# A third room for residual rows, a second for transposed probabilities, four other pairs for M, and tile 5's split between two exponentials

## The chip, the cores and the metric

The kernel runs on one core of one Trainium2 chip. A core has five engines, each working through its own list of instructions in order: TensorE (PE, with its weight loads, PEld), VectorE (DVE), ScalarE (ACT), GpSimd (POOL) and SyncE (SP), which here does little but issue DMAs. An engine that comes to an instruction whose operands are not there waits, and all that stands behind it in its list waits too. The metric is the device time of one execution in microseconds. Three runs before the change took 957.74, 960.12 and 963.96 us; the median is 960.12.

## What is computed

A block of four residual layers on x, 2 batches of 1024 tokens with 512 features, all in float32:

```python
x = x + attn_a(layernorm(x))    # gated linear attention in chunks of 128, 4 heads, state carried over chunks
x = x + ffn(layernorm(x))       # (silu(x Wg) * (x Wu)) Wd, hidden size 1408, integer weights with scales
x = x + attn_b(layernorm(x))    # softmax(Q K^T / sqrt(512)) V Wo, one head of width 512
x = x + ffn(layernorm(x))       # the same weights again
```

Of attention a, only the output is used. For each tile of 128 tokens it needs q, a normalised k and v, the decays from the gates, the scores inside the tile, and the state from the tiles before.

## The kernel before

**Tiles and precision.** The 2048 tokens are 16 tiles of 128. Matmuls take operands in a rounded form of float32 (fp32r). To keep float32 precision an operand is held as a high and a low part: `split` (lines 83 to 86) lets ACT cast to the high part and DVE, or POOL, subtract it from the source to get the low part. `mm3` (lines 97 to 103) then does three matmuls: high by high, high by low, low by high.

**Attention a** (lines 349 to 753). Before its loop the weights of attention b are folded into products: M from W_q and W_k at the start (`weight_product`, name "M"), and V from W_v and W_o near the end. M comes out of PE in four PSUM blocks. `spill` (line 181) splits each block and stores both parts in DRAM, where attention b fetches them; its tiles come from a pool under a given tag. Then q of four tiles (`q_head`, one head at a time), layer norms with transposes (`ln_tile`), and v of tile 0. The loop over 16 tiles does `kv_tile` (k and v of the next tile, tags sWk and sWv), `scores` (k transposed as kT, the state's update pd from kw and v, then the scores pS) and `chunk_out` (output of the tile before, with a residual row xra). `k_norm` and `k_factor` turn k into kw: square on ACT, sum on DVE, a power on POOL, factors on DVE, the product on POOL. `decay` reads a row from DRAM (`load_row`) and masks it on POOL.

**FFN** (line 756 on). Pairs of hidden blocks use a seven-product scheme with combined operands (B11, T1, T2 and so on, prepared from the transposed tokens by `combine`).

**Attention b** (lines 896 to 1187). For each batch, four cycles: `scores_head`, then work in between, then `scores_tail` with `softmax` for two tiles. `probs_T` transposes the probabilities: DVE transposes blocks of 32 by 32 into py, a DMA writes py to DRAM (p), four DMAs read it back placed into ptl, and `probs_split` splits it into pth and ptl for `out_b`. The tile before the last is transposed on PE instead (ppt). Tile numbers in the profile: tiles 8 to 15 belong to batch 1, so tile 13 is its tile 5.

**Order.** Tile pools hold a number of rooms (bufs) per tag, and a new tile takes the room of the one that many tiles before it; whoever writes it waits until the old tile's last user is done. Row tiles (tag xres) have two rooms, py one, sWk two. A scheduler in the program's builder puts each engine's instructions in order by its own estimate of times; `behind(...)` only says that a step is not to be issued ahead of given instructions. SP's list of DMAs is ordered in this way too, so a load whose room is not free holds up all later DMAs of SP.

## Time and profile before

| | us |
|---|---|
| median of three runs | 960.12 |
| profiled execution | 960.54 |
| its span, first to last instruction | 958.8 |
| PE busy in the span | 936.6 |
| DVE busy | 728.9 |
| ACT busy | 408.6 |
| POOL busy | 222.1 |

The profiled execution has 1.74 us around its span, and lies 0.42 us over the median. PE is busy for 98% of the span. Its matmuls overlap in the records: one of 128 by 512 lasts 0.39 us but the next starts 0.23 us after it. In the lists of waits a line names the waiting engine, tile and line, and what released it, with the total, the number and the longest wait. In the chain of work that ended last, a line has its start, its length, and the engine and tile. In the windows, a line gives for each engine the busy time and the number of instructions, then the granted clock of PE (1.00 is full), the DMA share and the rate in GB/s. A bracket at the end of a line of the timeline is idle time before it.

### The profile page before, as it was taken

How to read it: one execution, taken by the hardware profiler on the slowest of the kernel's cores; microseconds unless marked ns; L12 is line 12 of the kernel's file. 1: busy time of each engine (PE TensorE's matmuls, PEld its weight loads, DVE VectorE, ACT ScalarE, POOL GpSimd, SP SyncE). 2: the span in 40 equal slices, each digit the busy share in tenths (PEclk: the TensorE clock that was granted, in tenths of full speed). 3: DMA queues.
4: the chain of work that ended last, by engine and by line, in shares of the span. 5: the costliest groups of instructions: out<-in, count | busy, mean ns of one | idle time of the engine just before them, and what ended most of it. 6: DMA issues, size and time to landing. Idle time of an engine off the chain costs nothing.

```text
span 958.8 us, 13209 instructions
## 1 busy us (share of the span) xinstructions
PE 936.6 (98%) x4402; PEld 776.3 (81%) x4402; DVE 728.9 (76%) x1457; ACT 408.6 (43%) x793; POOL 222.1 (23%) x318
## 2 busy tenths in 40 slices
PE   8979999998899999999999999999999999999998
PEld 6768888887788878888888888888878888888887
DVE  7656767677999799787956897658975977976655
ACT  5543343425566443444324444234532444534421
POOL 6223322333464110210030400222400261001100
PEclk9999999999999999999999999999999999999999
DMA  8335546664798538652560787516877772573112
GB/s 298 110 132 140 167 112 185 178 150 148 290 387 245 170 124 310 183 150 67 198 216 12 165 198 173 190 22 132 195 173 235 280 209 52 180 263 132 39 59 96
DMA packets 215861, 162.18 MB, mean 169 GB/s; under 512 B 150960, under 2 KB 166640, under 8 KB 215792
## 3 DMA queue, kind: packets, MB, share of 16 engines
q1 hardware_dynamic: 213488, 156.61, 53.7%
q0 software_dynamic: 2304, 4.72, 2.3%
q8 instruction: 35, 0.57, 0.3%
q14 instruction: 34, 0.28, 0.1%
HBM read 104.76 MB, written 41.84 MB: 153 GB/s over the span
## 4 chain that ended last, share of the span: by engine, by line
PE 81%; DVE 7%; DMA 6%; ACT 2%; issue 1%; POOL 1%; SPq 1%; ACTq 0%; DVEq 0%; POOLq 0%
PE pog L868 4%; PE pog L867 4%; PE pZg L339 4%; PE pVg L339 4%; PE pXg L339 4%; PE pVf L339 4%; PE pZf L339 3%; PE pXf L339 3%; PE pob L100 3%; PE pof L867 3%; PE pob L98 3%; PE pob L99 3%; PE pof L868 3%; PE pYg L339 2%; PE psV L965 2%; PE psZ L965 2%
## 5 line engine op out<-in xcount | busy, mean ns | idle before, releaser
L867 PE MATMUL pog<-wdg,hsg 128*128 128x512 f32 (+1 forms) x165 | 60.1, 375 | 0.0
L868 PE MATMUL pog<-wdg,hsg 128*128 128x512 f32 (+1 forms) x165 | 60.1, 375 | 0.0
L868 PE MATMUL pof<-wdf,hsf 128*128 128x512 f32 x154 | 59.3, 390 | 0.8 <-DVE ve_b L121 0.8
L867 PE MATMUL pof<-wdf,hsf 128*128 128x512 f32 x154 | 59.1, 389 | 0.0
L98 PE MATMUL pob<-vh,pth 128*128 128x512 f32 x128 | 50.7, 396 | 1.2 <-ACT pth L85 1.2
L100 PE MATMUL pob<-vh,ptl 128*128 128x512 f32 x128 | 50.6, 396 | 0.7 <-DVE ptl L86 0.7
L99 PE MATMUL pob<-vl,pth 128*128 128x512 f32 x128 | 50.4, 394 | 0.0
L86 POOL TENSOR_TENSOR hsg<-sgg,hsg 128x128 fp32r<-128x128 f32 x40 | 17.6, 460 | 130.0 <-ACT hsg L85 130.0
L339 PE MATMUL pVg<-T_g,wcg 128*128 128x512 f32 x176 | 46.6, 389 | 0.0
L339 PE MATMUL pVf<-T_f,wcf 128*128 128x512 f32 x176 | 46.6, 389 | 0.0
L339 PE MATMUL pXg<-B_g,wcg 128*128 128x512 f32 x176 | 46.4, 389 | 0.0
L339 PE MATMUL pXf<-B_f,wcf 128*128 128x512 f32 x176 | 46.0, 390 | 0.3 <-DMA wcf<-wc 0.3
L123 POOL TENSOR_TENSOR rs_g<-ve_g,mhalf 128x1 f32<-128x1 f32 x16 | 13.2, 828 | 139.2 <-DVE ve_g L121 139.2
L123 POOL TENSOR_TENSOR rs_b<-ve_b,mhalf 128x1 f32<-128x1 f32 x16 | 11.3, 709 | 140.5 <-DVE ve_b L121 140.5
L211 POOL DMA_DIRECT2D xT_g<-y_g x48 | 30.9, 651 | 36.7 <-DVE T_b L86 28.7
L339 PEld LDWEIGHTS pXf<-B_f,wcf 128*128 128x128 f32 x176 | 32.9, 188 | 7.4 <-DMA wcf<-wc 0.7
L339 PEld LDWEIGHTS pVg<-T_g,wcg 128*128 128x128 f32 x176 | 33.0, 188 | 6.9
L339 PEld LDWEIGHTS pXg<-B_g,wcg 128*128 128x128 f32 x176 | 33.0, 188 | 6.9
L339 PEld LDWEIGHTS pVf<-T_f,wcf 128*128 128x128 f32 x176 | 33.0, 188 | 6.9
L867 PEld LDWEIGHTS pog<-wdg,hsg 128*128 128x128 f32 x165 | 31.1, 188 | 5.7
L868 PEld LDWEIGHTS pog<-wdg,hsg 128*128 128x128 f32 x165 | 31.0, 188 | 5.6
L868 PEld LDWEIGHTS pof<-wdf,hsf 128*128 128x128 f32 x154 | 28.9, 188 | 7.2 <-DVE hsf L86 1.2
(334 smaller groups left out, 2740.4 us busy)
## 6 DMA issues: line engine op xcount, KB each, us to landing
wcg<-wc SPq DMA_DIRECT2D x22, 896.0 KB, 6.3
wc<-wcf SPq DMA_DIRECT2D x11, 896.0 KB, 5.2
wcf<-wc SPq DMA_DIRECT2D x11, 896.0 KB, 6.0
p<-py SPq DMA_DIRECT2D x15, 512.0 KB, 3.7
ptl<-p SPq DMA_DIRECT2D x56, 128.0 KB, 3.0
xin_a<-in_x SPq DMA_DIRECT2D x16, 256.0 KB, 4.0
xra<-in_x SPq DMA_DIRECT2D x16, 256.0 KB, 2.7
row<-cl SPq DMA_DIRECT2D x16, 256.0 KB, 3.6
```

The source lines that it names most:

```text
L86: return c.ins, (eng or nc.vector).tensor_tensor(lo, src, hi.bitcast(F32), ALU.subtract).ins
L98: nc.tensor.matmul(ps, lhs_hi, rhs_hi, start=first, stop=False)
L99: nc.tensor.matmul(ps, lhs_hi, rhs_lo, start=False, stop=False)
L100: end = nc.tensor.matmul(ps, lhs_lo, rhs_hi, start=False, stop=last).ins
L123: nc.gpsimd.tensor_tensor(rs, ve, mhalf, ALU.pow)
L211: (nc.sync if sync else nc.gpsimd).dma_start(out=xf[32 * b : 32 * (b + 1), :, c, :], in_=y[32 * c : 32 * (c + 1), b].rearrange("p k i q -> ...
L339: nc.tensor.matmul(ps, w[:, m, k * P : (k + 1) * P], o[:, s, k, :], start=first and k == 0 and s == 0, stop=k == 1 and s == 1, skip_group_ ...
L867: nc.tensor.matmul(ps, hs[i][0][:, j], wd[j][:, ds], start=j == 0, stop=False)
L868: nc.tensor.matmul(ps, hs[i][1][:, j], wd[j][:, ds], start=False, stop=j == KH - 1)
L965: ends[nm] = nc.tensor.matmul(ps, o[:, i, k], w[:, j, k], start=first and k == 0 and i + j == 0, stop=k == 1 and i == 1, skip_group_check= ...
```

## The change

Eight things are altered.

1. Residual rows get a pool of their own with three rooms, for all four layers.
2. py gets two rooms instead of one.
3. `spill` of M uses the tags kT, kw, sdec and at (two rooms each) instead of sWk.
4. The layer norms of tiles 4 to 7 stand behind the q heads: none after the first, then 4, 5, and 6 with 7.
5. For batch 1's tile 5, `probs_split` moves out of the cycle into `scores_tail`, after the first tile's softmax; the second tile's exponentials are to stand behind its casts.
6. Two steps of the second FFN's operands (`do(moving, 2)`) move from ahead of the last cycle into it.
7. s3 takes the room of u2; the gate tile ab gets one room.
8. Constants used by attention a alone go into attention a's pool.

```diff
+    rp = ctx.enter_context(tc.tile_pool(name="rows", bufs=3))
...
-        xin = xp.tile([P, D], F32, tag=tag, name=f"xin_{name}")
+        xin = (rp if tag == "xres" else xp).tile([P, D], F32, tag=tag, name=f"xin_{name}")
...
-            ab = ap.tile([48, 512], F32R, tag="ab", name=f"ab{st}")
+            ab = a1.tile([48, 512], F32R, tag="ab", name=f"ab{st}")
...
-            xr = xp.tile([P, D], F32, tag="xres", name=f"xra{t}")
+            xr = rp.tile([P, D], F32, tag="xres", name=f"xra{t}")
...
-        spill(ap, ("sWk",), pm, m_d, "M")
+        spill(ap, ("kT", "kw", "sdec", "at"), pm, m_d, "M")
         for i in range(4):
+            ends.clear()
             q_head(0, i)
-            with behind((wq_loaded,)):
-                ln_tile(4 + i)
+            with behind((wq_loaded, *ends.values())):
+                for t in ((), (4,), (5,), (6, 7))[i]:
+                    ln_tile(t)
...
-            s3 = b1.tile([P, 2, P], F32, tag="s3", name=f"s3_{b}{n}")
+            s3 = b1.tile([P, 512], F32, tag="u2", name=f"s3_{b}{n}")
+            s3 = s3[:, 0:256].rearrange("p (k c) -> p k c", k=2)
...
             softmax(b * NK + 2 * n, (X, Z))
-            softmax(b * NK + 2 * n + 1, (V, up))
+            casts = []
+            if (b, n) == (1, 3):
+
+                casts = probs_split(1, 5, last)
+            softmax(b * NK + 2 * n + 1, (V, up), casts)
...
             for s, x in enumerate(halves):
-                act = nc.scalar.activation(
-                    pe[:, s * 512 : (s + 1) * 512], x, AF.Exp, bias=nm, scale=SC, accum_out=rs[:, s : s + 1]
-                )
+                with behind(casts):
+                    act = nc.scalar.activation(
+                        pe[:, s * 512 : (s + 1) * 512], x, AF.Exp, bias=nm, scale=SC, accum_out=rs[:, s : s + 1]
+                    )
...
-            y = b1.tile([P, T], F32, tag="py", name=f"py{t}")
+            y = bp.tile([P, T], F32, tag="py", name=f"py{t}")
...
                 for i in (2 * n - 2, 2 * n - 1):
-                    probs_split(b, i, summed)
+                    if (b, i) != (1, 5):
+                        probs_split(b, i, summed)
...
-            if b:
-                do(moving, 2)
-            else:
+            if b == 0:
                 moving = combine("b", 1)
                 do(moving, 1)
-            cycle(b, 3, lambda: out_b(b, 3))
+
+            def between():
+                out_b(b, 3)
+                if b:
+                    with behind(summed):
+                        do(moving, 2)
+
+            cycle(b, 3, between)
```

The row tiles of the FFN (xrf, xrg) and of attention b (xrb) change in the same way as xra. The scheduler orders the changed program anew, so instructions stand elsewhere too where no line was edited.

More of the change, by code (lines that the diff above doesn't have):

```diff
@@ L55, in hybrid_block_kernel @@
     make_identity(nc, ident)
-    ones = cp.tile([P, P], F32, name="ones")
-    nc.gpsimd.memset(ones, 1.0)
-    le = cp.tile([P, P], F32, name="le")
-    nc.gpsimd.affine_select(
-        out=le, in_=ones, compare_op=ALU.is_ge, fill=0.0, base=0, pattern=[[1, P]], channel_multiplier=-1
-    )
-    gt = cp.tile([P, P], F32, name="gt")
-    nc.vector.tensor_tensor(gt, ones, le, ALU.subtract)
-    fold_f = cp.tile([48, 8], F32, name="fold_f")
-    nc.vector.tensor_reduce(
-        fold_f, ident[0:48, 0:64].rearrange("p (a b c) -> p c a b", a=2, b=4)[:, :, :, 0:2], AX.XY, ALU.add
-    )
-    fold = cp.tile([48, 8], F32R, name="fold")
-    nc.vector.tensor_copy(fold, fold_f)
     mhalf = cp.tile([P, 1], F32, name="mhalf")
@@ L353, in hybrid_block_kernel @@
         sp = actx.enter_context(tc.tile_pool(name="stage", bufs=4))
+        ones = a1.tile([P, P], F32, name="ones")
+        nc.gpsimd.memset(ones, 1.0)
+        le = a1.tile([P, P], F32, name="le")
+        nc.gpsimd.affine_select(
+            out=le, in_=ones, compare_op=ALU.is_ge, fill=0.0, base=0, pattern=[[1, P]], channel_multiplier=-1
+        )
+        gt = a1.tile([P, P], F32, name="gt")
+        nc.vector.tensor_tensor(gt, ones, le, ALU.subtract)
+        fold_f = a1.tile([48, 8], F32, name="fold_f")
+        nc.vector.tensor_reduce(
+            fold_f, ident[0:48, 0:64].rearrange("p (a b c) -> p c a b", a=2, b=4)[:, :, :, 0:2], AX.XY, ALU.add
+        )
+        fold = a1.tile([48, 8], F32R, name="fold")
+        nc.vector.tensor_copy(fold, fold_f)
         normed, key_copy, late_norm = {}, [], []
@@ L858, in ffn @@
                             done = h_split(n, js, ha[:, n - 2, js] if n < ST else hb[:, n - ST, js], None)
-                    xr = xp.tile([P, D], F32, tag="xres", name=f"xr{nm}{t}")
+                    xr = rp.tile([P, D], F32, tag="xres", name=f"xr{nm}{t}")
                     nc.sync.dma_start(out=xr, in_=src[t])
@@ L993, in scores_tail, with softmax @@
             softmax(b * NK + 2 * n, (X, Z))
-            softmax(b * NK + 2 * n + 1, (V, up))
-        def softmax(t, halves):
+            casts = []
+            if (b, n) == (1, 3):
+                casts = probs_split(1, 5, last)
+            softmax(b * NK + 2 * n + 1, (V, up), casts)
+        def softmax(t, halves, casts=()):
             mx = mp.tile([P, 2], F32, tag="mx", name=f"mx{t}")
@@ L1004, in softmax @@
             for s, x in enumerate(halves):
-                act = nc.scalar.activation(
-                    pe[:, s * 512 : (s + 1) * 512], x, AF.Exp, bias=nm, scale=SC, accum_out=rs[:, s : s + 1]
-                )
+                with behind(casts):
+                    act = nc.scalar.activation(
+                        pe[:, s * 512 : (s + 1) * 512], x, AF.Exp, bias=nm, scale=SC, accum_out=rs[:, s : s + 1]
+                    )
             ri = mp.tile([P, 1], F32, tag="ri", name=f"ri{t}")
@@ L1053, in probs_split @@
             hi, lo, raw, _ = ptT[b * NK + i]
+            casts = []
             with behind(after):
@@ L1057, in probs_split @@
                     done = split(hi[:, ks], lo[:, ks], raw[:, ks])
+                    casts.append(done[0])
                     if b * NK + i == NT - 3:
                         splits.extend(done)
+            return casts
         def out_b(b, i):
@@ L1063, in out_b @@
             hi, lo, _, ri = ptT[t]
-            xr = xp.tile([P, D], F32, tag="xres", name=f"xrb{t}")
+            xr = rp.tile([P, D], F32, tag="xres", name=f"xrb{t}")
             nc.sync.dma_start(out=xr, in_=x2[t])
```

## Prediction

> **What bounds the kernel now.** I read the first part of the page, then who TensorE (PE) waited for, then the chain that ended last around the longest wait, and last the windows with the granted clock.

> ```profile
> span 958.8 us, 13209 instructions
> ...
> PE 936.6 (98%) x4402; PEld 776.3 (81%) x4402; DVE 728.9 (76%) x1457; ACT 408.6 (43%) x793; POOL 222.1 (23%) x318
> ```

> The matmuls themselves are untouched, so only the 22.2 us in which PE is idle, and slow stretches inside its busy time, can move. The waits of PE are few:

> ```profile
> PE pd L605 <- POOL kw L582: 6.3, 2, 4.4
> PE pl L639 <- DVE at L624: 2.5, 1, 2.5
> PE pkT L592 <- DVE sWk L546: 1.3, 1, 1.3
> PE pob L98 <- ACT pth L85: 1.2, 1, 1.2
> ```

> The columns are total us, times, longest us. By place these are three holes: 64 to 71 us (1.30 and 4.42), 229 to 251 us (1.86, 0.98 and 2.53, from the timeline), and 714 to 717 us (1.22 and 0.74). The chain says what made the first; it is M on its way out:

> ```profile
> 55.84 3.49 DMA m<-M
> ...
> 62.85 1.97 DMA m<-M
> ...
> 64.91 0.69 DVE sWk L546
> ...
> 69.64 1.05 POOL kw L582
> ...
> 70.73 2.08 PE pd L605 x8
> ```

> M's blocks pass one after the other through the two sWk rooms (a third store, left out, is at 60.02); each block waits for the store before it, and tile 1's k (sWk) stands behind the last. k's norm, the POOL power and kw follow before pd can run. Note the 2.08 us for eight pd: the same eight take 0.89 us at 85.33. The windows give the reason:

> ```profile
> 64.36:70.73 6.37, 0.66 (x5) 0.42 (x5) 5.38 (x14) 3.64 (x5) 3.06 (x4) 0.89 0.37 125
> 70.73:76.22 5.49, 5.49 (x25) 5.49 (x26) 3.85 (x11) 2.56 (x8) 4.49 (x6) 0.51 0.38 102
> 712.92:717.72 4.80, 2.83 (x14) 1.79 (x14) 4.33 (x10) 4.80 (x11) 0.00 (x0) 1.00 0.27 91
> 717.72:721.50 3.78, 3.78 (x11) 2.99 (x10) 3.75 (x5) 0.11 (x1) 0.00 (x0) 0.55 0.74 199
> ```

> Third number from the end is the granted clock: after each of these two holes PE runs at about half clock for 4 to 5 us.

> **M through four other pairs of rooms.** In the order in which the changed kernel stands, all four splits of M come right after its product, at about 19 to 26 us, and sWk1 has its room free when pWk1 ends (50.2). Walked with the rows' durations: sWk1, sq1 behind dec0 on ACT (to 56.0), the reduction behind at0 (57.3), POOL's power (58.5), s2 (59.5), kw1 (60.6). PE reaches pd1 at 64.8, so 4 us are to spare. Ahead of pS1 stands kT1 on ACT, and the new order has two more table loads there (1.28 us each): e at 59.7, load, lu, load, dec1, load, la, kT1 done at 65.9. PE wants it at 66.6, after 4 pkT (0.44), 8 pd and 8 pl (0.89 each). That spare of 0.7 us is the thinnest of the stage; if the cover is gone it costs up to the 2.6 us of the loads. I take 0. Gain, from start to start: the last pWv starts at 63.96 and the first pq after the scores at 75.87; without holes and at full clock it is 63.96 + 0.23 + 0.44 + 3 x 0.89 = 67.3. Gain 8.6 us: 5.7 idle, 2.8 slow clock.

> **What that costs at the start.** VectorE is full from 16 to 32 us (8.00 and 7.91 of 8 in those windows). Four M splits (0.68 each, less at its usual overlap: 2.5) now stand before tile 4's statistics, and tile 0's ss (0.67) before xn_a4, so xn_a4 ends at 28.7 + 3.2 = 31.9 instead of 28.7. But ln_tile(4) is now behind q_head(0, 1), whose 12 matmuls (2.7 us) PE does first: it asks at 30.8 where it asked at 27.9. The wait is 1.1 against 1.02 now. Bounds: none at all, or 3 us if ACT's four casts (0.58 each) hold Wq too; I take +0.1. Wv's four loads stand behind eight stores of M on SP's queue, at 26.5 instead of 23.57; its first product is at 39.4, and the last cast comes at 37.9, against 32.2. Cover 1.5 us; 0.

> **Third room for rows.** SP waits 18.8 us in all for stores of xra and 14.7 for xrb, which looks like much. But the new order issues each load one tile earlier, after the same store: xra14 stands where xra13 stood, and takes the room of xra11, the same tile. So row 15's load still sits behind a load that waits for x1_11, whose store took 6.12 us from 217.15. The second hole stays. Bounds: a gain of 5.4 (1.86 + 0.98 + 2.53) or a loss of 0.5; I take 0, since every step of its chain stands in the old order.

> **Two rooms for transposed probabilities, tile 5's split between the exponentials.** The third hole in the timeline:

> ```profile
> 712.92 1.31 PE L1027 MATMUL ppt<-ident,pe 128*128 128x128 f32 x8
> ...
> 714.78 1.13 ACT L85 CAST pth<-ptl 128x512 fp32r<-128x512 f32 x2
> ...
> 715.45 0.50 PE L98 MATMUL pob<-vh,pth 128*128 128x512 f32 x1 [1.22 <-ACT pth L85]
> ```

> The cast for tile 13 comes after four exponentials. In the changed order it comes after two. Will its data be there? p_4 goes no earlier (696.70: again a row load waits 3.07 us for the store ahead of it). But py13 needs no longer wait for p_4's landing, so p_5 goes at 697.1 instead of 703.32, and the four loads of ptl13 follow those of ptl12 as pob11 frees their room, at 703.3 to 705.7 instead of 707.10 to 709.50; landed by 708.7 (3.01 us as ptl12). On DVE, one subtraction for the FFN (1.21) has moved behind the maxima: exponentials of tile 14 end at 708.6, pth13 at 709.9, those of 15 at 711.4, ptl13 at 711.2. PE wants both at 714.1, after the transposes. The first wait (1.22) and the second (0.74) go, with 3 us to spare.

> What is late next: ptl14 at 717.1, wanted at 719.6; for pob15, py15 at 713.8, p_7's landing at 717.0 (3.05), raw's four issues to 720.4 (3.42), landed by 723.4, the cast's first half 724.0, the first low half 724.6; wanted at 725.0. I allow 0.3. Then T3 (727.8) for the FFN, wanted at 733.

> Size from start to start: 712.92 to 738.18 is 25.3 us; 8 transposes (0.9) and 88 matmuls at 0.2267 are 20.9 or, with the pipeline's turn, 21.1. Gain 4.2, of which the slow clock is 1.6 (nine starts from 717.72 take 3.65 instead of 2.04). [...]

> **At nothing:** one ab buffer (read last near 32, written again at 44.80); s3 in u2's room (u2's last reader is on DVE before s3's writer, and the next copy into it comes a scores tail later); constants in another pool (the same POOL instructions, behind them PE's 1.21 us start: 0 to 0.2); tile 4 to 7 regrouped; both further q and p transfers in attention b, where no PE wait was found and the cover is 10 us or more.

> **Sum.** 8.6 + 4.2 - 0.1 - 0.3 = 12.4 us. The profiled execution took 960.54 with its 1.74 around the span, the median of the runs is 960.12: 947.7.

> **Rivals.**
> - *Only M's hole closes* (16%). Something else holds pob13 or pob15: most likely raw's loads, which share the DMA engines with the FFN weights. Speaks for it: spare under 1 us. 960.1 - 8.5 = 951.6.
> - *The start pays* (8%). VectorE and ScalarE are late with Wq and xn_a4 by 5 us, with a slow clock after it: 952.7. For: the full windows. Against: PE's order puts 2.7 us of cover in between.
> - *The change does more than its parts: hole two closes as well* (6%): 947.7 - 5.4 = 942.3. Against: xra14 and row 15.
> - *Slower* (4%). The early cast for tile 13 stands in ACT's order before tile 15's exponentials. If its loads are late, they, py15, p_7, raw and pob15 all wait behind it. It has 3.7 us until VectorE would notice (712.4), then each us is one; the hole's own gain is gone at a landing of 717, and the kernel is slower from 725 on, 16 us past my landing. At 730, 965. No row of a ptl load is near that.

> **Numbers.** Both holes close: 66%, 947.7, itself 945 to 950. The range of 944 to 953 reaches to the first rival and most of the second. The three runs lie 6 us apart, so 1% (9.6 us) is what can be told from no change. Faster by more than that: nearly all of the 66%, the 6%, none to a third of the 16%: 0.72. Slower 0.03, within 0.25.

> **What would show it.** PE's 4.42 and 1.30 gone, granted clock 1.00 from 60 to 80; pxT_a still about 1; pob's waits gone and 1.00 after them; 1.86, 0.98 and 2.53 still there; p_5 right behind p_4 on SP. I am wrong if pkT or pS waits for kT1, if pob15 waits for raw, or if the granted clock falls elsewhere.

## The result, and the profile after

Six runs of the changed kernel gave 952.59 us in the median (951.10 to 953.06) against 958.93 (957.68 to 963.96) of six runs of the kernel before on the same chip: the two medians lie 6.3 us apart. The ratio of all runs, which is not that of the medians (0.9934), is 0.9922, with a 95% interval of 0.9897 to 0.9948. A later repetition gave 0.9927 (0.9910 to 0.9944). So the change saves 6 to 7.5 us, a little over half of the 12.4 that I had summed. The profiled execution took 951.10 with a span of 949.4; it is the fastest of its six, and the one of before was slower than its median, so the two profiles lie 9.4 us apart. Below, places are compared by profile, and sizes by all runs.

From the page of the changed kernel, its span and busy times:

```profile
span 949.4 us, 13214 instructions
...
PE 935.0 (98%) x4402; PEld 775.8 (82%) x4402; DVE 725.2 (76%) x1457; ACT 412.0 (43%) x795; POOL 219.1 (23%) x318
```

PE's idle time fell from 22.2 to 14.4 us. What PE waited for in the changed kernel (total us, times, longest us):

```profile
PE pob L83 <- ACT pth L70: 2.5, 1, 2.5
PE pl L640 <- DVE at L625: 2.2, 1, 2.2
...
PE pxT_a L118 <- DVE xn_a L110: 1.0, 3, 0.4
...
PE pS L621 <- ACT kT L595: 0.7, 1, 0.7
PE pd L606 <- POOL kw L583: 0.5, 1, 0.5
```

The 4.4 and the 1.3 of M's hole are gone, and the wait of 1.2 for pth as well. But there is a new first line: pob waits 2.5 us for pth, and this is another tile, 12 and not 13. (A number behind a name is the tile: pob12 is the output product of tile 12. Only p counts within the batch: p_4 is the transfer that writes tile 12's transposed probabilities to DRAM, p_5 that of tile 13, p_7 that of tile 15.) Where the time changed hands is best seen from the starts of some PE groups (us; the difference is the changed kernel minus before):

| PE reaches | before | changed | difference |
|---|---|---|---|
| first pWv | 39.55 | 38.85 | -0.7 |
| first pl | 72.6 | 64.9 | -7.7 |
| first pq behind the hole | 75.9 | 66.6 | -9.3 |
| last pq | 194.1 | 185.7 | -8.4 |
| first pXf | 251.9 | 243.0 | -8.9 |
| last psX (first of its six) | 703.3 | 693.8 | -9.5 |
| first ppt | 712.9 | 708.0 | -4.9 |
| last pog | 954.7 | 945.2 | -9.5 |

The start and M's hole bring everything. Of their 9.3 us, 0.9 is lost again by the last pq. Between the last psX and the first ppt 4.6 us are lost: 2.5 is pob12's wait, and 2.0 is that pob12 then takes 7.43 us up to the first ppt where it took 5.45. From there on 4.5 us are won back by the absence of the old waits. Over the third hole, from the last psX to the last pog, the kernel before takes 251.4 us and the changed one 251.5.

PE at the first hole, from the changed kernel's timeline (start, duration, group):

```profile
63.31 0.39 PE L85 MATMUL pWv<-Wv,xl_a 128*128 128x512 f32 x1
63.54 0.60 PE L593 MATMUL pkT<-ident,sWk 128*128 128x128 f32 x4
63.98 1.06 PE L606 MATMUL pd<-sWv,kw 128*128 128x128 f32 x8
64.87 1.06 PE L640 MATMUL pl<-sWv,at 128*128 128x128 f32 x8
65.76 1.06 PE L621 MATMUL pS<-qT,kT 128*128 128x128 f32 x8
66.58 0.48 PE L83 MATMUL pq<-xh_a,Wq 128*128 128x512 f32 x1
```

From the last pWv to the first pq it is 66.58 - 63.31 = 3.27 us, where the kernel before needed 75.87 - 63.96 = 11.91. The third hole is now one tile earlier. First the chain around tile 12 in the kernel before, where PE reached pob12 at 707.47 and did not wait:

```profile
696.70 4.10 DMA p<-py
...
702.54 3.01 DMA ptl<-p
...
705.62 0.63 ACT pth L85
```

Then the chain in the changed kernel, and its windows with the granted clock as the third number from the end:

```profile
695.53 3.95 DMA ptl<-p
...
699.91 0.63 ACT pth L70
...
700.58 0.50 PE pob L83
```

```profile
698.02:701.43 3.41, 0.94 (x4) 0.42 (x4) 0.87 (x2) 1.52 (x3) 0.00 (x0) 1.00 1.58 147
701.43:704.85 3.42, 3.42 (x9) 2.65 (x10) 2.42 (x7) 2.66 (x8) 0.00 (x0) 0.50 0.42 90
```

PE wants tile 12's probabilities at 698.1, their cast ends its first half at 700.5, and after the wait the clock falls to half. The next-to-last column is the DMA engines' share, 1.58 in the hole (packet times are added up, so it can pass 1). What SP issues there (start, time of the group):

```profile
684.81 0.32 SPq L1082 DMA_DIRECT2D x<-xrb  x1
688.92 0.32 SPq L1077 DMA_DIRECT2D xrb<-x  x1
689.33 1.23 SPq L1045 DMA_DIRECT2D p<-py  x2
693.72 5.93 SPq L1056 DMA_DIRECT2D ptl<-p  x8
```

A row load stands 4.1 us behind the store of x3_10; only then p_4 goes, with p_5 at its heels, and then both tiles' eight loads in one go. In the kernel before, p_5 went only at 703.32, behind tile 12's four loads, and tile 13's loads at 707.10.

### The profile page after: what moved, and what is told of

It reads as the page before. It is cut to its first block, busy times and chain, and to the rows that moved or that the text cites. A ratio compares the mean times of both kernels' runs of the same rounds, so it can differ in the third digit from the quotient of the medians.

```text
span 949.4 us, 13214 instructions
## 1 busy us (share of the span) xinstructions
PE 935.0 (98%) x4402; PEld 775.8 (82%) x4402; DVE 725.2 (76%) x1457; ACT 412.0 (43%) x795; POOL 219.1 (23%) x318
## 3 DMA queue, kind: packets, MB, share of 16 engines
q1 hardware_dynamic: 213488, 156.61, 56.6%
## 4 chain that ended last, share of the span: by engine, by line
PE 86%; DVE 5%; DMA 3%; SPq 2%; ACT 2%; issue 1%; POOL 1%; ACTq 0%; POOLq 0%; DVEq 0%
PE pXf L324 4%; PE pog L871 4%; PE pog L870 4%; PE pZf L324 4%; PE pVg L324 4%; PE pVf L324 4%; PE pZg L324 4%; PE pXg L324 4%; PE pof L871 3%; PE pof L870 3%; PE pob L85 3%; PE pob L83 3%; PE pob L84 3%; PE psV L969 2%; PE psZ L969 2%; PE psX L969 2%
## 5 line engine op out<-in xcount | busy, mean ns | idle before, releaser
L85 PE MATMUL pob<-vh,ptl 128*128 128x512 f32 x128 | 50.8, 397 | 0.0
L108 POOL TENSOR_TENSOR rs_b<-ve_b,mhalf 128x1 f32<-128x1 f32 x16 | 11.6, 728 | 141.6 <-DVE ve_b L106 137.4
L108 POOL TENSOR_TENSOR rs_g<-ve_g,mhalf 128x1 f32<-128x1 f32 x16 | 9.6, 604 | 137.9 <-DVE ve_g L106 137.9
L196 POOL DMA_DIRECT2D xT_g<-y_g x48 | 30.9, 652 | 40.5 <-DVE T_b L71 29.0
```

What stands on the lines that cost most here:

```text
L85: end = nc.tensor.matmul(ps, lhs_lo, rhs_hi, start=False, stop=last).ins
L108: nc.gpsimd.tensor_tensor(rs, ve, mhalf, ALU.pow)
L196: (nc.sync if sync else nc.gpsimd).dma_start(out=xf[32 * b : 32 * (b + 1), :, c, :], in_=y[32 * c : 32 * (c + 1), b].rearrange("p k i q -> ...
```

## The experiments

My theory after the result: M's rooms and the regrouped norms bring the whole gain; the tail won its old waits and lost as much to tile 12's transfers, which are late against PE and share the DMA engines with tile 13's. Rivals: one edit alone is at fault (the split between the exponentials, the third room), or p_4's place on the queue alone. All ratios are to the kernel before, measured beside each. The kernel before took 958.8 to 961.4 us beside them, and the times that were expected count from 958.9, so they are compared by ratio. The scheduler orders each of these kernels anew, so an edit can move other instructions too.

| run | what it is | median us | ratio (95%) |
|---|---|---|---|
| 1 | before + M's rooms | 956.10 | 0.9955 (0.9935 to 0.9975) |
| 2 | changed, p_4 before xrb13 | 954.13 | 0.9928 (0.9911 to 0.9944) |
| 3 | changed, ptl13 later | 958.05 | 0.9970 (0.9957 to 0.9983) |
| 4 | changed, row 15 before xra14 | 951.50 | 0.9899 (0.9883 to 0.9915) |
| 5 | before + M's rooms + norms | 951.28 | 0.9901 (0.9866 to 0.9935) |
| 6 | changed, split put back | 951.50 | 0.9910 (0.9882 to 0.9938) |
| 7 | changed, one py room | 960.36 | 0.9996 (0.9984 to 1.0008) |
| 8 | one py room, p_4 and row 15 first | 957.08 | 0.9961 (0.9948 to 0.9974) |
| 9 | changed, two rooms for rows | 950.58 | 0.9908 (0.9889 to 0.9927) |
| 10 | changed, p_4 first, p_5 behind ptl12, split put back, row 15 first | 950.32 | 0.9912 (0.9895 to 0.9929) |
| 11 | changed, again | 952.31 | 0.9927 (0.9910 to 0.9944) |
| 12 | run 10, FFN steps behind tile 13's split | 948.06 | 0.9894 (0.9875 to 0.9914) |

### Run 1: M's rooms alone

```diff
-        spill(ap, ("sWk",), pm, m_d, "M")
+        spill(ap, ("kT", "kw", "sdec", "at"), pm, m_d, "M")
```

> The kernel before with one line changed: M leaves through the four other pairs of rooms; norms stay grouped as before. If M's hole is worth what the trace of before says (5.7 us of waits and 2.8 of slow clock) and nothing else of the change matters there: 950 to 951.5 us against 958.9, no PE wait of 4.4 or 1.3 us, granted clock 1.00 from 60 to 80 us; both waits of pob for pth (1.22 and 0.74) either as before or shorter, since nothing moved there. If the regrouping of tiles 4 to 7 is needed for it (four more splits on VectorE ahead of tile 4's norm): a wait of pxT_a of 3 us or more and 953 to 956.

PE's waits in run 1:

```profile
PE pxT_a L133 <- DVE ve_a L121: 3.5, 1, 3.5
...
PE pd L605 <- POOL kw L582: 1.1, 1, 1.1
```

The hole at 64 us is gone (first pWv to first pl takes 26.0 us as in the changed kernel, 33.0 before), and in its place PE stands 3.5 us at 27 to 31 us for tile 4's norm, because VectorE now has four splits of M ahead of it; the granted clock is 0.50 from 30 to 36 us. First pWv comes at 44.1 instead of 39.6. So the rooms win 7.0 us and pay 4.5 of them at the start: the second theory's price, and its time (0.9955 of 958.9 is 954.6).

### Run 5: M's rooms and the regrouped norms

```diff
-        spill(ap, ("sWk",), pm, m_d, "M")
+        spill(ap, ("kT", "kw", "sdec", "at"), pm, m_d, "M")
         for i in range(4):
+            ends.clear()
             q_head(0, i)
-            with behind((wq_loaded,)):
-                ln_tile(4 + i)
+            with behind((wq_loaded, *ends.values())):
+                for t in ((), (4,), (5,), (6, 7))[i]:
+                    ln_tile(t)
```

> The kernel before with M's four other pairs of rooms and the regrouped norms of tiles 4 to 7, nothing else of the change. If M's hole is closed by these two together as the trace of the changed kernel suggests, and the rest of the change is worth nothing or costs: 0.990 to 0.992 of before (950 to 951 us where before is 958.9), no pxT_a wait over 1.1 us, no PE wait of 4.4, and pob's waits of 1.22 and 0.74 about as before. If the regrouping has a price of its own later (tiles 6 and 7 come late): 0.994 or more, with a wait between 40 and 60 us.

As the first theory expected: 0.9901, first pWv at 39.0, first pl at 65.0, and both old waits of the third hole (1.2 and 0.7) still there with a half clock behind them. PE's waits in run 5:

```profile
PE pob L98 <- ACT pth L85: 1.2, 1, 1.2
...
PE pxT_a L133 <- DVE xn_a L125: 0.9, 3, 0.4
```

These two edits together give what the whole change gives, if not a little more. All the other edits, taken together, are worth nothing that can be measured.

### Run 6: the split put back

```diff
-            if (b, n) == (1, 3):
-
-                casts = probs_split(1, 5, last)
...
-                    if (b, i) != (1, 5):
-                        probs_split(b, i, summed)
+                    probs_split(b, i, summed)
```

> The changed kernel with tile 13's split put back ahead of all four exponentials' order as before (behind the sums of the scores' head, not between the exponentials); both py rooms stay. If pob12's wait comes from the transfers (p_5 beside p_4, ptl13 beside ptl12): it stays at 2.3 to 3.3 us, and the time within 1.5 us of the changed kernel (0.991 to 0.9935 of before). If the split between the exponentials is what delays tile 12: the wait falls under 1 us and the time to 0.989 or less.

The wait of pob12 stays at 2.4 us and the time is that of the changed kernel (0.9910). With two rooms, tile 13's cast follows the four exponentials at 706.12 and is still in time for PE. So the split between the exponentials is neither the cause of the new wait nor a gain.

### Run 7: one room for transposed probabilities

```diff
-            y = bp.tile([P, T], F32, tag="py", name=f"py{t}")
+            y = b1.tile([P, T], F32, tag="py", name=f"py{t}")
```

> The changed kernel with one room for the transposed probabilities instead of two, so p_5 waits again until p_4 has landed, and ptl13 for p_5; the split between the exponentials stays. If sharing the DMA engines with tile 13's transfers (p_5 first of all) is the main cause of pob12's wait: p_4 lands about 4.1 us after its issue, ptl12's last load 3.0 us after its own, the wait falls from 2.5 to between 0 and 1.2 us; 0.988 to 0.9905 of before, less up to 1.5 us if tile 13's cast, later now, holds the exponentials of tile 15. If p_4's late issue is the cause: wait 2 us or more, 0.992 or more.

Neither theory had the time: it is that of the kernel before. pob12's wait did fall, to 1.64 us, but two others came. PE's waits in run 7:

```profile
PE pXg L324 <- DMA wcg<-wc: 3.4, 1, 3.4
PE pob L83 <- ACT pth L70: 3.4, 2, 1.8
```

SP's queue in run 7 shows why:

```profile
696.72 0.73 SPq L1045 DMA_DIRECT2D p<-py  x1
...
711.54 0.37 SPq L1045 DMA_DIRECT2D p<-py  x1
...
715.60 2.35 SPq L1056 DMA_DIRECT2D raw<-p  x4
...
718.92 1.43 SPq L313 DMA_DIRECT2D wcg<-wc  x3
```

Tile 13's cast (707.65) stands on ScalarE before tile 15's exponentials (708.68), and these are late already (tile 14's at 706.32, run 5: 704.55), because in this order VectorE has tile 12's subtraction ahead of the maxima and tile 12 is late. So py15's transfer p_7 goes at 711.54, where run 5, which also has one room but its split behind the exponentials, sends it at 708.74. raw and the FFN's weights wcg stand behind p_7 on SP: PE waits 1.78 for tile 15 and then 3.44 for wcg, and the granted clock is 0.50 to 0.71 from 722 to 730 us. This is the mechanism of my "slower" rival, with wcg at its end that the rival did not name, at a size of 7 us against the changed kernel. The second room is what keeps the split between the exponentials from paying that: the room without the split is run 6, worth nothing that can be measured, and the split without the room costs 7 us. One room without the split, in the rest of the changed kernel, was not run; run 5, which has that but lacks the other edits too, pays nothing of the kind.

### Run 3: tile 13's loads later

```diff
-            nc.sync.dma_start(out=x3[t], in_=xr)
+            stored = nc.sync.dma_start(out=x3[t], in_=xr).ins
+            if t == 11:
+                with behind((stored,)):
+                    later[0]()      # tile 13's four ptl loads
```

> The changed kernel with tile 13's four loads (ptl13) issued behind the store of x3_11, near 697.5 instead of 696.7, so that ptl12's four have the DMA engines to themselves while they are issued; p_5 stays where it is. If sharing the engines with ptl13's is the whole cause of pob12's wait: ptl12 lands 2.9 to 3.0 us after its issue, the wait of 2.47 goes to under 0.5, 949 to 949.5 us. If sharing is only one of several delays (p_4 stands late behind the store, too): the landing goes from 4.0 to about 3.0, the wait to about 1.4, 950.5 to 951.5 us. If it isn't sharing at all: wait 2.3 to 2.6, 952.6 us.

None of the three fits. pob12 waited 3.23 us: p_4 took 5.3 us to land, with p_5 still beside it, and tile 12's last load took 3.96 us, no less than with tile 13's loads close behind (3.95). Tile 13's loads, from 697.99 on, overlapped its landing after all, so this run does not acquit them; it shows that moving them by one us is no cure. The long time (0.9970) has what run 7 showed in its trace: tile 13's cast was later (704.61, against 703.15), the new order has the FFN's first products inside pob15, and pXg waited 3.3 us for wcg.

### Runs 2, 8, 10 and 12: the order on SP's queue

Run 2 puts p_4 ahead of the row load:

```diff
+            with behind([written[12]] if t == 13 else ()):     # written[12]: p_4
-            nc.sync.dma_start(out=xr, in_=x2[t])
+                nc.sync.dma_start(out=xr, in_=x2[t])
```

> The changed kernel with tile 13's residual row (xrb13) issued behind p_4 instead of before it, so p_4 no longer stands behind the landing of the store of x3_10 (4.1 us). If lateness of p_4 is what makes pob12 wait 2.47 us: p_4 goes near 685.2 instead of 689.3, ptl12's cast is done near 696, PE asks at 698.1; the 2.47 us and the slow clock behind it (about 1.5 us) go: 948.6 us. If another wait takes its place (p_5 still stands behind the same store; tile 13 or the exponentials become late): 951 to 952.6, with a pob or ppt wait of 1.5 us or more.

The wait did not go but grew to 3.24 us, in a time (0.9928) like that of the changed kernel. p_4 could only go once py12 was turned, 2.1 us behind the store instead of 4.5, and then landed after 6.7 us instead of 4.3, with xrb13 and p_5 issued within 2 us of it and the POOL queue still issuing xT_g (until 691.0). Run 8 does the same with one room, so without p_5 beside it, and has row 15 of run 4:

> One room for the transposed probabilities, xrb13 issued behind p_4, xra14 behind row 15's load. If lateness and sharing are both parts of pob12's wait: p_4 goes as py12 is done (about 2.4 us earlier against PE), alone; ptl12's cast is done before PE asks and the wait is gone with its slow clock, 0.986 to 0.989 of before (946 to 949 us where before is 958.9). If the landing of p_4 is set by other traffic (the POOL queue's xT_g transfers, xrb13): it takes 5 us or more, a wait of 1 us or more stays, 0.990 to 0.992.

pob12's wait fell to 0.33 us although p_4 took 6.0 us to land; the price of one room (1.37 at pob15, 2.4 for wcg) stayed, and with 0.9961 the time is outside both ranges. Run 10 keeps both rooms and orders p_5 behind tile 12's four loads, with the split behind the exponentials:

```diff
+            with behind([brought[12]] if t == 13 else ()):     # brought[12]: tile 12's last load
-            written[t] = nc.sync.dma_start(
+                written[t] = nc.sync.dma_start(
```

> The changed kernel with two rooms for transposed probabilities kept, but on SP's queue p_4 before xrb13 and p_5 only behind tile 12's four loads; tile 13's split behind the exponentials; xra14 behind row 15. If p_5 beside p_4 is what stretched tile 12's landing, and in the runs with one room the loss came from tile 13's cast standing before tile 15's exponentials and from the FFN's weights behind raw: pob12's wait under 0.6 us, no pXg wait for wcg, pob15's wait under 0.5, 0.984 to 0.987 of before (943.5 to 946.5 us where before is 958.9). If tile 13, now as late as with one room, makes PE wait at pob13 instead: 1 to 2 us there with a slow clock, 0.988 to 0.991.

pob12's wait was 0.43 and nothing waited for wcg, but PE stood 1.57 us at pob13, the second theory's place and nearly its time (0.9912), though without its slow clock: VectorE had the FFN's T1 ahead of tile 13's low half. Run 12 takes that away:

```diff
-                    with behind(summed):
+                    with behind([*summed, *splits]):
                         do(moving, 2)
```

> As the run before (p_4 before xrb13, p_5 behind tile 12's loads, split behind the exponentials, xra14 behind row 15), with the two FFN steps that stand there (T1's difference and split) put behind tile 13's split on VectorE and ScalarE. In the run before, PE waited 1.57 us at pob13 for ptl13's low half, which VectorE had behind T1's split (1.20 us). If that order is all that is left of the third hole: both pob waits 0.5 us or less, granted clock 1.00 from 697 to 715, 0.987 to 0.990 of before. If tile 13's loads themselves are late now: pob13's wait 1 us or more, 0.990 to 0.992. If the FFN's T1 or B22 are late instead: a wait of pXg or pVg of 1 us or more near 720, 0.990 to 0.993.

pob13's wait is gone, as expected, but in the profiled execution p_4 took 6.8 us to land, and pob12 waited 1.78 us again, with half clock behind it from 698.3 to 701.8. So the ordering does not close the third hole safely. At 948.06 us (0.9894) this is still the fastest kernel of the study: 0.3% under the changed one, with intervals that just overlap, and part of it may be row 15 (run 4).

All fourteen profiles side by side on tile 12. "Lead" is from p_4's issue to PE's asking for pob12, "p_4" from its issue to tile 12's first load, which waits for its landing, "loads" from there to the cast. The cast's first half takes another 0.7 us until PE can go, so where PE waits, the wait is the sum plus 0.7 less the lead:

| kernel | p_5 right behind p_4 | p_4 issued while POOL still issues xT_g | lead us | p_4 us | loads us | sum | pob12 waits |
|---|---|---|---|---|---|---|---|
| before | no | just ending | 10.8 | 4.15 | 4.77 | 8.9 | 0 |
| run 1 | no | no | 10.6 | 4.18 | 4.85 | 9.0 | 0 |
| run 5 | no | no | 10.2 | 4.24 | 5.27 | 9.5 | 0 |
| run 7 | no | no | 8.8 | 4.21 | 5.59 | 9.8 | 1.64 |
| changed | yes | no | 8.8 | 4.39 | 6.19 | 10.6 | 2.47 |
| run 11 | yes | just ending | 9.8 | 4.79 | 6.04 | 10.8 | 1.71 |
| run 4 | yes | no | 8.7 | 5.08 | 5.97 | 11.0 | 3.00 |
| run 6 | yes | no | 9.6 | 5.45 | 5.87 | 11.3 | 2.38 |
| run 3 | yes | no | 9.0 | 5.40 | 6.19 | 11.6 | 3.23 |
| run 9 | yes | yes | 9.7 | 5.79 | 5.53 | 11.3 | 2.25 |
| run 2 | yes | yes | 10.8 | 6.76 | 6.61 | 13.4 | 3.24 |
| run 10 | no | yes | 11.4 | 5.63 | 5.54 | 11.2 | 0.43 |
| run 8 | no | yes | 12.1 | 6.01 | 5.73 | 11.7 | 0.33 |
| run 12 | no | yes | 11.3 | 6.88 | 5.56 | 12.4 | 1.78 |

Two things make up the 2.47. One is lateness: PE comes to pob12 9.4 us earlier than before (698.1 against 707.5), p_4 goes only 7.4 us earlier (689.33 against 696.70), and the 2.0 us between them are more than the 1.2 that tile 12 had to spare. The other is p_5 and ptl13 beside tile 12. The first four sums average 9.3 us, the next five 11.1, but the kernels differ in more than p_5; the closest pair, run 7 against the changed kernel, has the same lead, and sums of 9.8 and 10.6. So PE waits 1.64 us there without p_5, and 0.8 more with it; each is a single execution. More than that, up to the 1.7 of the averages, is possible and not shown. Where p_4 was sent earlier (runs 2, 8, 10 and 12), it landed slower. The third column suggests that this is xT_g's doing, but in these four runs xrb13's load, too, follows p_4 within 3 us; a run that separates the two was not made.

### Run 4: row 15 ahead of tile 14's residual row

```diff
+            with behind([rowl[15]] if t == 14 else ()):        # rowl[15]: row 15's load
-            nc.sync.dma_start(out=xr, in_=x_in[t * P : (t + 1) * P, :])
+                nc.sync.dma_start(out=xr, in_=x_in[t * P : (t + 1) * P, :])
```

> The changed kernel with tile 14's residual row (xra14) issued behind row 15's load instead of before it; row 15 then stands only behind the issue of x1_11's store (207.0), not its landing (213.5). If that landing is what the second hole comes from, as my prediction had it: row 15 issues near 207.7 instead of 213.9, PE's waits of 0.53 at 221, 1.02 at 230 and 2.22 at 241 us go for the most part, 949 to 950 us. If the wait at 241 us comes from POOL's own work (the wcf conversions stand before s2 there), only the 0.53 goes: 952 us, and 2.0 to 2.3 us remain at 241.

Between the two: the time (0.9899 of 958.9 is 949.2) is the first theory's, the large wait the second's. In the changed kernel xra14 stood 6.5 us behind the store of x1_11, and row 15 behind it; now row 15 goes at 211.71 and not at 213.93, so 2.2 us of the 6.2 that were expected. Yet pd's wait for kw near 221 us is gone from the list in all four kernels with this order (runs 4, 8, 10, 12); in all the others it is there, with 0.2 to 1.9 us. PE's waits of run 4:

```profile
PE pl L641 <- DVE at L625: 2.5, 1, 2.5
...
PE pV L84 <- DVE V L71: 0.9, 1, 0.9
```

The 2.5 us near 240 stay. From the last pq to the first pXf it is 56.0, 57.5, 55.5 and 55.0 us in these four, against 57.3 and 56.6 in the two profiles of the changed kernel and 55.9 in run 9, whose wait for kw happened to be 0.2. These overlap, so about one us, the size of pd's wait, is all that can have been won, and the large wait there is not row 15's. In the changed kernel's chain the POOL steps of the FFN's first weights (wcf, 0.7 to 1.2 us each) stand directly ahead of k's power there; taking them away was not tried.

### Run 9: two rooms for rows

```diff
-    rp = ctx.enter_context(tc.tile_pool(name="rows", bufs=3))
+    rp = ctx.enter_context(tc.tile_pool(name="rows", bufs=2))
```

> The changed kernel with two rooms for the residual rows instead of three. If the third room is worth nothing, since each load then waits one tile later for the same store (the step as the prediction had it): same time as the changed kernel within 1 us (0.991 to 0.993 of before), waits of pd for kw between 0.5 and 1.9 us, pob12's wait of 2.4 to 3 us unchanged. If the third room is what shortened pd's wait from 1.86 to 0.53: about 1.3 us longer, 0.994. If the third room makes xrb13 stand in front of p_4 and is part of pob12's wait: 1 us or more shorter with a wait under 1.5 us.

Nothing lost: 0.9908, pd's wait 0.2, pob12's 2.25. The third room is worth nothing that can be measured, as predicted, and is not what shortened pd's wait.

### Run 11: the changed kernel again

> The changed kernel itself again, as the measure for the other runs of this call: 0.991 to 0.9935 of before, pob12's wait 2.3 to 3.2 us.

0.9927. pob12 waited 1.71 us here, a little under what was expected, and the wait at 241 us was 2.35.

## Why the prediction was right or wrong, step by step

**M's hole: right to 0.1 us.** I had 8.6 from the last pWv to the first pq; the trace shows 11.91 - 3.27 = 8.64. The thin spare of 0.7 us for kT1 held: it was done at 64.94, and pS follows at 65.76 without a wait. (A later tile pays: pS waits 0.75 for kT at 91.72, which it did not before.)

**The start: right, by more than I said.** I took +0.1 and measured -0.7. PE asked for tile 4's norm at 30.8, as I had it, but VectorE was done with it at 30.9 and not at 31.9, so the wait was 0.2 and not 1.1. Run 1 shows what that regrouping is worth: 5 us. The second rival ("the start pays") is exactly what happens without it.

**The third room: right at 0** (run 9). The second hole stayed as said, with 1.6 us of waits less than before (1.86, 0.98 and 2.53 became 0.53, 1.02 and 2.22). Its cause was only half right: row 15 behind the store accounts for about one us (run 4), not for the wait near 240.

**The third hole: wrong, because tile 12 was put at nothing.** I sent p_5 right behind p_4 and tile 13's four loads right behind tile 12's, gave them the old duration ("landed by 708.7 (3.01 us as ptl12)"), and then asked what is late among tiles 13, 14 and 15 alone. What I did walk came true: it came so on the queue, tile 13 was in time, the old waits of 1.22 and 0.74 went, and from the first ppt to the last pog 4.5 us were won where I had 4.2 less 0.3. But tile 12, which PE needs first, lost as much, 2.47 us of wait and 2.0 us of slower matmuls behind it. The old duration did not hold: with tile 13's transfers in flight, p_4 and tile 12's loads took 10.6 to 11.6 us together instead of 8.9 to 9.8, and the last load of tile 13 took 4.26 us instead of 3.01. And I walked the tail in the old kernel's times, where the first half of tile 12's cast was done (706.24) 1.2 us before PE asked. After M's hole PE asks 9.4 us earlier, and p_4 followed by only 7.4, so that spare was gone before p_5 took anything, as run 7 shows with its wait of 1.64. The part that I put at 4.2 less 0.3 came out at about 0 to 1.5 us (from the last psX to the last pog 251.5, 250.7 and 249.9 in the two profiles of the changed kernel and in run 9, 251.4 before).

**The clock: not a fixed part of the hole.** I counted 1.6 us of slow clock into this hole, since the trace of before shows 0.55 behind it. Run 6 has a wait of 2.38 us there with a granted clock of 1.00 throughout, the changed kernel 0.50 behind 2.47. Nor was it half clock "for 4 to 5 us" before: by the clock's own records it was 6.83 us at M's hole (69.27 to 76.10) and 3.41 at the third (717.80 to 721.22). The last section has what the traces show of it.

**The rivals.** The time is that of the first, "only M's hole closes" (951.6), but not for its reason: in the changed kernel neither pob13 nor pob15 waited, and raw held up nothing. The mechanism of "slower" is real (run 7), and in the changed kernel only the second room holds it off. "Hole two closes as well" did not come, with 2.22 us left near 241.

**The sum.** The front brings 8.6 + 0.7, which run 5 gives as 9.5 (0.9901 of 960.62; 6.2 to 12.9 by its interval). The changed kernel's 7.0 to 7.5 by the same kind of ratio would make the rest of the change a loss of 2 to 2.5 us, but the intervals overlap: shown is only that it gains nothing. I had 947.7, itself 945 to 950. The measured 952.59 is inside the range of 944 to 953 by luck: the range went so far for rivals whose reasons did not come about. And the gain, 0.7 to 0.8%, did not pass the 1% for which I had given a chance of 0.72.

## What to carry to other kernels

When one change closes an early hole and another re-orders transfers at a late one, walk the late one again with the engine that sets the pace shifted by the early gain: transfers that wait for stores and for other transfers need not shift with it (here PE came 9.4 us earlier and p_4 7.4). A second room for a staged tile (one on its way through DRAM) also lets the next tile's transfers start beside this one's (here p_4 and tile 12's loads took 10.6 us with two rooms and 9.8 with one, changed kernel and run 7); ask first which of the two is wanted first, and cost the first one with the other in flight. And an operation put earlier into an in-order queue to save a wait is only as safe as the latest landing it can see: here, with one room, it went with 7 us when its tile's cast came 4.5 us later.

## What the runs showed of the hardware that I had not expected

Whether PE's clock falls after a hole is not told by the length of the hole. In these traces a single wait of 1.71 (run 11, at 699), 1.78 (run 12), 2.12 (run 9, at 240), 2.22 and 2.47 us (changed kernel) was followed by a granted clock of 0.50, and a wait of 1.57 and 2.30 (run 10), 2.12 (run 12, at 239), 2.25 (run 9, at 700), 2.35 (run 11, at 241), 2.38 and 3.06 us (run 6) by none.

```profile
697.90:701.31 3.41, 2.36 (x11) 1.55 (x9) 1.78 (x4) 0.00 (x0) 0.00 (x0) 1.00 1.23 160
701.31:704.73 3.42, 2.09 (x8) 1.44 (x9) 2.08 (x5) 2.48 (x6) 0.00 (x0) 1.00 1.42 177
```

In the last step ahead of a fall PE was idle for 2.96 us at M's hole before, 1.80 at the third hole before, 2.05 near 241 us in the changed kernel, and 1.64 at pob12 in run 7. The 2.53 us at 251 before lay in two steps with 1.93 and 0.60, and the clock stayed at 1.00. So 1.64 and 1.80 us idle in a step were followed by half clock and 1.93 were not; what decides is not shown. In the two profiles of the changed kernel the clock fell behind pob12's wait at 701.43 and at about 700.9 (run 11), and the hole near 241 us was followed by 0.50 in the first and by 1.00 in the second. For a sum of this kernel it means that the slow clock behind a hole of about 2 us is a chance and not a term: one step at half clock, 1.7 us as an estimate from its 3.41, or nothing.
